# Output sums, row statistics and late norms moved between engines, scratch in PSUM, and another instruction order in a hybrid attention block

## Chip, cores and metric

The kernel runs on one core of a Trainium2 chip. The metric is the device time of one execution in microseconds (us); lower is better. A core has five engines that run their own instruction queues in order and wait for each other by semaphores: TensorE (PE; its weight loads are shown as PEld), VectorE (DVE), ScalarE (ACT), GpSimd (POOL) and SyncE (SP), which issues nearly all transfers here.

## What is computed

The reference applies four layers to `x` of shape 8 x 512 x 128, each added to its input after a layer norm over the 128 features. All is float32.

```python
x = x + attn_a(layernorm(x))   # delta rule, 16 heads of 8
x = x + ffn(layernorm(x))      # 8 experts, best 2 per token
x = x + attn_b(layernorm(x))   # linear attention, elu + 1, 16 heads of 8
x = x + ffn(layernorm(x))      # the same weights again

# attn_a: q, k, v = silu(short_conv(x @ W.T)), 4 taps; beta = sigmoid(x @ Wb.T)
# q, k divided by their norms over the 8 features of a head; then, token by token,
v_new = (v_t - k_t @ S) * b_t
S = S + outer(k_t, v_new)
o_t = q_t @ S
# o * rsqrt(mean(o * o) + eps) * o_norm_w, then @ Wo.T

# ffn: probs = softmax(x @ Wg); two largest, divided by their sum, as weights
h = relu(einsum('nd,edf->enf', xt, W1))    # 128 -> 256
y = einsum('enf,efd->end', h, W2)          # 256 -> 128
out = einsum('ne,end->nd', combine, y)

# attn_b: q, k = elu(x @ W.T) + 1; causal, with running sums S and z
out = (A @ v + q @ S) / (A.sum(-1) + q @ z + eps)   # A = tril(q @ k.T)
```

## The kernel before

**Tiling.** The 512 tokens of the eight sequences are cut into eight chunks `c` of 64 tokens. A chunk holds 64 tokens of all 8 sequences: 512 rows, kept as a tile of 128 partitions x 4 x 128 features. Chunk 7 goes through the later layers as two halves (`HALVED`).

**Stages of a chunk.** `prepare` (from L815) loads and normalizes the chunk, transposes it, projects it to q, k, v and beta, takes the short convolution (chunks 0 to 3 as four accumulated matmuls, later ones as three VectorE instructions for each of q, k, v, `s_pp_a<-cv_a`), and regroups the result to one sequence and head per partition through scratch in DRAM (`scr`, `qk`, `vv`). Norms of q and k come from `norms_of` (L877): squares on ScalarE, sums over a head by `over_heads` (four strip matmuls `s_pn_a`, a copy, a store `scn` and a load `nrm`), a clamp on GpSimd. `back` (L1020) and `substituted` (L1080) solve the delta rule within four steps, with a scratch tile `spare` and the result `W`.

`recurring` (L1176) is the sequential part: 16 steps per chunk, each of four VectorE instructions (`pj`, `factors`, `terms`, `st`). After every four steps `outputs` (L1235) multiplies the kept states by the queries on GpSimd (`po`, four instructions of 256 elements) and sums over the 8 features on VectorE (`o<-po`, 1024 to 128 elements); `SUMS_ON_PE`, empty here, names the chunks that would use TensorE instead. `ending` (L1296) corrects and normalizes the outputs (`on`) and sends them through DRAM (`sco`, `oT`) to be projected (`s_po_a`) and added to `x`.

`moe` (L1446) is a feed-forward layer, `f` the first and `g` the second. It transposes the rows, computes the routing logits (`narrow`, L778: four strip matmuls, one for each 128 tokens, then a copy and one transpose back), and then the routing on VectorE up to the weights `cb`. `relative` (L1518) turns the difference of the two largest logits into two weights with Exp. `all_experts` (L1354) sends `cb` to DRAM (`s_pw`, `cT`, `scw`), loads a row of it to all partitions for each expert (`wt_xsT<-scw`, 256 KB), multiplies by the transposed rows on GpSimd, and runs 16 matmuls `s_ph` with Relu on ScalarE (`hT`) and 16 accumulating matmuls `y_py`, all 512 wide. Expert 0 of chunks 0 and 7 is scaled before the transpose instead (`TURNED_IN`) and needs no load.

`linear_attention` (L1791) and `attend` (L1573) are attn_b. The row means come from strip matmuls (`s_pm_b`), a copy and a transpose, the variances from ScalarE squares (`inverse_deviation`, L760).

**Order.** Each engine's order is fixed when the program is built. A planner (`Weaver`, L153 on) runs all stages as streams against a table of durations (`duration`, L444) and at each step takes the stream whose remaining chain, plus a constant of its own from `FAVOURED` and `OFFSETS`, is longest. `PASSES` says how often the chains are computed anew. The first-come slots of `Slots` (L335) hand out tiles: five general PSUM banks (`banks`, L617), two for the feed-forward's sums and logits (`long_banks`), one for the recurrence. `keep_busy` (L1874) places filler matmuls (`busy`, L1885) of a matrix of ones in free banks where the planner sees TensorE idle for 0.6 us or more.

Every instruction issued through the planner has the line of its helper, L430, in the profile, so that the tiles' names are the way to read it. The expert weights 5 to 7 are loaded to `resident` only after chunk 3's projections, as their tiles hold the convolution's weights until then.

Of the kernel before, what the change touches and what calls it, by code (L numbers as in the profile page):

```python
# [42 lines left out]
SUMS_ON_PE = ()  # L43
# [3 lines left out]
ADDED_ON_DVE = (4,5,6,7)  # L47
KEPT_ON_DVE = (4,5,6)
# [14 lines left out]
PASSES = ((1, 0.0, {}), (17, 0.1, {}))  # L63

FAVOURED = {
    ("b", 0.0): 847, ("b", 1.0): -301, ("b", 2.0): 48, ("b", 3.0): -4, ("b", 4.0): -976, ("b", 5.0): -1159,
    ("b", 6.0): 509, ("b", 7.0): -2460, ("b", 7.5): 186, ("beside",): -125, ("ending",): 1282, ("f", 0):
    164, ("f", 1): -235, ("f", 2): -208, ("f", 3): 29, ("f", 4): 931, ("f", 5): -141, ("f", 6): -314, ("f",
    7): 1886, ("f", 7.5): -1425, ("g", 0.0): -218, ("g", 1.0): 61, ("g", 2.0): -140, ("g", 3.0): 611, ("g",
    4.0): 1326, ("g", 5.0): 199, ("g", 6.0): -1053, ("g", 7.0): -2296, ("g", 7.5): 1775, ("outputs",): -478,  # L70
    ("prepare", 0): -2816, ("prepare", 1): 490, ("prepare", 2): -322, ("prepare", 3): -911, ("prepare", 4):
    77, ("prepare", 5): -24, ("prepare", 6): 83, ("prepare", 7): -370, ("recur", 0): 2489, ("recur", 1):
    -593, ("recur", 2): 572, ("recur", 3): -1791, ("recur", 4): -302, ("recur", 5): -833, ("recur", 6):
    -3302, ("recur", 7): -653, ("values",): -814, None: -170,
# [4 lines left out]
    -94, -63, 10, -192, -39, 12, -114, -698, -137, 154, 81, -154, 130, -7, 6, -2, -25, -22, -2, 171, -146,  # L79
    -7, -70, 86, -128, -1, 17, -350, 642, -227, 85, -53, -408, -72, 354, -37, 34, -6, 645, -20, -144, 59,  # L80
    149, 52, 49, 18, 421, -76, -46, -60, 563, -491, 107, 160, -7, 102, -88, 28, 57, 480, -125, -15, -198,
    -41, -6, 81, 85, 0, 8, 24, -159, -105, 12, 78, -58, -26, -244, 80, -179, -12, 37, -10, 146, 131, 114,
    61, -165, 199, 28, 153, 232, 126, 187, 3, -64, -4, -68, -5, 154, -129, 405, 149, -77, -184, -114, 6,
    140, 71, 0, -30, 398, -30, 199, 51, 201, -31, -7, 93, 86, 98, 175, 3, 134, -160, 32, -8, 65, 39, 184,
    172, 22, -195, 62, -6, -117, -193, -21, 224, -2, 11, 349, 84, 127, 214, 76, -14, 19, -519, 30, 4, -176,
    -6, -26, -64, -20, 294, -16, -87, -219, 1, -473, -50, 39, -21, -282, -34, -184, 97, 149, -21, -158,
    -104, 106, 72, 0, 119, 19, 141, 62, 112, -108, 0, -120, -72, -44, 5, -107, -26, 0, -99, 88, 131, 88, 51,
    102, -9, -406, -123, 20, -48, -420, 9, 139, 52, -694, 192, 164, 383, 181, 63, 80, -29, 128, 63, 1, 144,
    196, 1, -34, 91, -132, -127, -70, 192, -19, -32, 65, 136, 236, 52, -67, -1, 15, -90, -28, 0, 2, 22, -94,
    -96, -15, 0, -15, -22, 99, 3, -43, -150, 46, 133, -168, 9, 53, 3, -72, 8, -173, 449, 96, 28, 122, -136,  # L90
    422, -272, 7, 434, 221, 71, -7, 29, -29, 153, 229, 84, -129, 5, 23, 279, 24, -90, -194, -16, -56, 427,
    89, -3, 1, -11, -603, -381, 204, 67, -10, -5, 0, -2, 45, -263, -472, -138, 30, 30, 82, 194, -1, -59,
    -23, -58, 0, 108, 62, -9, 5, -88, -5, -7, 18, -109, -19, 111, -199, -12, -202, 0, 89, 481, 420, -6,
    -211, 70, 51, -263, -17, 39, 141, 71, 4, -55, -254, 179, -98, 103, 36, -265, 132, -34, -36, -47, 41, 94,
    0, 12, -1, 146, 300, -7, 142, -45, 316, 3, -167, 2, -187, -134, -82, -567, 4, 37, 118, -22, 201, 80, 39,
    67, 63, -32, 260, -167, -29, -70, -55, -469, -372, -49, -2, 236, 0, 295, 102, 7, -41, 74, 9, -134, 43,
    -34, 188, -24, 140, -5, 429, 11, -94, 28, -42, 5, -15, -118, 87, -61, 20, 0, 475, 5, 16, -69, -126, 319,
    4, -99, 69, -4, 70, -87, 176, -124, -24, 435, 195, -54, 82, -79, 4, 720, -20, 54, 32, -167, 634, 242,
    -96, -30, -407, -108, -261, 56, -137, -130, 0, -300, 368, 33, 288, -490, 1, 22, -94, 42, 243, -58, 151,
    -49, 22, -272, 31, 845, 96, 0, 187, 208, -186, 12, 81, 23, -3, -487, -1188, 112, 246, 12, -243, -20,  # L100
    -207, 131, 0, 9, 1, 92, -154, -51, 0, -12, 174, 34, -129, 4, 60, 110, 27, 22, 67, -71, -22, -42, 59,
    210, 19, -55, 55, -152, 9, -15, -11, -151, 5, 0, -27, -47, 90, 461, 19, -340, -125, -548, -9, -32, -230,
    -61, -263, -69, 106, 281, 208, 173, 130, 24, -453, -25, -527, -530, 71, 63, 3, -54, 215, -207, 22, -48,
    -658, 219, 71, -172, -353, 11, -68, 60, -249, 0, 50, -22, 150, 6, -350, -52, 76, 30, -35, 557, 232,
    -368, -37, 275, -101, 150, 23, 282, 0, -780, 68, -85, 129, -425, 631, 106, 15, -121, 71, 30, 13, 0,
    -328, -24, 9, -98, -460, -5, -51, -90, 2, 20, 20, -105, -38, 87, 1, 0, -199, 99, 32, 89, 41, -98, 1,
    -272, -19, 2, -52, 181, 141, 243, 28, -31, -49, -72, 7, -71, -40, -24, 87, 8, -8, -51, -124, -5, 90,
    -63, -99, 264, 34, -87, 1, 92, 68, 55, -26, 299, -407, -12, 25, -346, 18, -21, -6, 44, 257, 0, 260,
    -223, -60, -27, 184, 47, 635, 14, -534, 0, 140, -70, -304, 223, 34, -48, 62, -166, -8, -102, -78, -30,
    103, -30, -960, -162, -66, -29, 50, -158, 711, 29, 291, 43, 14, 7, 92, -303, 27, 45, -809, 107, -64,  # L110
    138, 122, 0, -66, -98, -85, -58, 16, -414, -177, 106, -114, 45, 57, 51, 411, -98, -32, 16, 73, 321,
    -511, -85, 0, 397, 113, 54, 411, -4, 1, -51, 47, 414, 2, 166, 15, 92, 69, 58, -247, 30, 262, -1, 52,
    -212, -4, 18, -74, 98, 9, 30, -177, -203, -9, 10, 157, 31, 18, 29, -52, -10, -148, -8, 94, 228, 279, 77,
    2, 378, 636, -57, 159, 585, -108, -19, 247, 111, 562, 391, -2, 225, 13, -402, 143, -89, -146, -22, -185,
    -20, 132, -42, -70, 158, 1, 50, 37, -28, -167, -90, -210, 121, -233, -10, -66, 169, 191, 46, 36, -32,
    164, 68, 148, 540, -107, -33, -181, -38, -203, -36, 0, -147, 24, -545, -18, 89, -120, -91, -112, 569,
    -397, 90, -431, 640, -64, 17, -78, 12, -574, 0, 63, 16, -348, 271, 0, -12, -338, -270, -117, 29, -320,
    -188, -665, -232, 187, 43, -42, 130, -48, 66, -174, 22, 45, 51, 89, 11, 282, -21, 205, 433, -88, 263,
    -183, -149, 23, 0, -165, 22, -19, 116, 253, -89, -42, 80, 25, 8, -96, -35, -48, 22, 77, -33, 140, -44,
    0, -9, 65, -18, 87, 134, 104, 110, -25, 201, 0, 489, -110, 111, 35, 132, 96, 21, 26, 27, -33, -16, 10,  # L120
    20, -47, 28, 31, -10, -346, -6, 31, 72, -31, -124, 209, -70, 57, -329, -2, 164, 72, 25, 111, -22, -8,
    105, 297, 3, -394, 4, -68, 112, 104, 271, -203, 0, 2, 222, 24, 3, -55, -276, 94, -36, -222, -39, -139,
    41, 5, 126, -154, 82, 59, 40, 219, -79, 31, 117, 101, -104, -163, 0, -21, 140, 75, 13, 14, 27, 122, 63,
    201, -21, 0, 0, -86, -38, 79, -230, 330, 101, -77, 169, -15, -63, -74, 205, 6, -5, 11, 52, -8, -66, -5,
# [8 lines left out]
TABLES = ("exp", "silu", "sqrt")  # L133
TABLE_OF = {AF.Exp: "exp", AF.Tanh: "exp", AF.Silu: "silu", AF.Sqrt: "sqrt"}
# [24 lines left out]
class Weaver:  # L159
# [24 lines left out]
    def took(self, engine, us, lag=0.1, table=None, lands=0.0):  # L184
        free = self.clock.get(engine, 0.0)
        if engine == "PE":
            if table != self.mode:
                self.mode = table
                free += MODE
        elif table and table != self.table:  # L190
            self.table = table
            free += 1.3
# [68 lines left out]
    def run(self):  # L261
# [3 lines left out]
        def start(s):  # L265
            at, was_on, lag = s.state[:3]
            if isinstance(s.on, Event):
                return max(at + lag, s.on.at)
            engine = "ACT" if s.on in TABLES else s.on
            free = self.clock.get(engine, 0.0)  # L270
            switch = SWITCH if s.on in TABLES and s.on != self.table else 0.0
            at += lag if was_on != engine else after(engine)
            return max(at + switch, free + switch) if PENALTY else max(at, free + switch)
# [170 lines left out]
def duration(key, op, args, kw):  # L444
    if op == "dma_start":
        return key, 0.4, 0.0, None, LANDS
    if key == "PE":
        mode = args[0].shape[0], args[2 if op == "matmul" else 1].shape[0]
        mode = None if mode == (P, P) else mode
        if op == "transpose":  # L450
            return key, 0.115, 0.2, mode
# [42 lines left out]
def merged(  # L494
# [106 lines left out]
    nc.gpsimd.memset(mhalf, -0.5)  # L601

# [32 lines left out]
    hTs = held_in(3, [P, HB * P], "hT")  # L635
# [142 lines left out]
    def narrow(out, w, src, n):  # L778

        for g in range(n):  # L780
# [3 lines left out]
            if g:  # L784
                weaver.overlaps(0.15)

    def halves(out, w, src):

        for g in range(4):
# [3 lines left out]
            if g:  # L793
                weaver.overlaps(0.15)
# [1149 lines left out]
```

## Time and profile before

| what | value |
|---|---|
| median of three runs | 811.18 us (807.44, 811.18, 811.40) |
| the profiled execution, its time | 810.49 us |
| the profiled execution, first to last instruction (span) | 808.8 us |
| TensorE clock granted, mean | 0.973 |
| filler matmuls among TensorE's 757.4 us | 61.7 us, 227 matmuls |
| 512-wide expert matmuls, back to back | 0.86 us each |
| activation table loads | 30, 1283 ns each |

The page cuts the span in 40 slices of 20.2 us. In its second part each digit is the busy share of an engine in tenths, and PEclk is the clock that TensorE was granted:

```profile
DVE  1689997897999999889878897997625625442410
ACT  5665758767765667686857766766455555555443
POOL 1243545468658666774674668376805644446241
PEclk9998997799999999999999999999999999999999
```

VectorE is nearly full from the third slice to the fifteenth, and falls off after the recurrence of the last chunk, at some 560 us. In the groups of the profile, a line gives engine, operation, out and in tiles, shapes, the number of instructions, then total busy time, the mean of one, and the idle time of the engine ahead of them with what ended it.

### The profile page before, as it was taken

What the parts mean: (1) busy time and instruction counts of PE and PEld (TensorE: products, weight loads), DVE (VectorE), ACT (ScalarE), POOL (GpSimd) and SP (SyncE); (2) the same over time, 40 slices, a digit from 0 to 9 for tenths busy, and PEclk for the clock granted to TensorE, in tenths of its full rate; (3) what the DMA queues carried; (4) which work ended last, traced back from release to release, by engine and by line L of the source; (5) the groups of instructions that cost most, each with busy time, mean ns of one, the idle gap of its engine ahead of it and who ended that gap; (6) DMA issues with size and microseconds to landing.
All of it is one profiled execution on the core that took longest, in us unless ns stands there. A gap on an engine that the chain in (4) does not pass through costs nothing.

```text
span 808.8 us, 11447 instructions
## 1 busy us (share of the span) xinstructions
PE 757.4 (94%) x3321; PEld 371.3 (46%) x3321; DVE 575.2 (71%) x1425; ACT 512.3 (63%) x1434; POOL 446.0 (55%) x595
## 2 busy tenths in 40 slices
PE   8897895799888999999989999999999999999997
PEld 4343342343333444444534444444456545644476
DVE  1689997897999999889878897997625625442410
ACT  5665758767765667686857766766455555555443
POOL 1243545468658666774674668376805644446241
PEclk9998997799999999999999999999999999999999
DMA  2442442415521030222423224231401301303120
GB/s 45 118 124 52 125 106 59 125 40 132 133 65 55 1 94 25 80 79 80 118 72 91 93 45 141 70 106 37 108 1 47 106 21 39 106 1 99 40 76 23
DMA packets 84839, 60.24 MB, mean 74 GB/s; under 512 B 50600, under 2 KB 66600, under 8 KB 84776
## 3 DMA queue, kind: packets, MB, share of 16 engines
q1 hardware_dynamic: 84056, 59.23, 26.5%
q8 instruction: 26, 0.43, 0.2%
q10 hardware_dynamic: 720, 0.28, 0.2%
q14 instruction: 37, 0.30, 0.1%
HBM read 46.71 MB, written 12.78 MB: 74 GB/s over the span
## 4 chain that ended last, share of the span: by engine, by line
PE 71%; DVE 18%; ACT 3%; POOL 3%; issue 3%; DMA 2%; SPq 0%; DVEq 0%; ACTq 0%; POOLq 0%
PE s_ph_g L430 13%; PE y_py_g L430 13%; PE s_ph_f L430 11%; PE y_py_f L430 10%; PE s_pc_b L430 4%; PE s_pp_a L430 3%; PE busy L1885 3%; DVE spare L430 2%; DVE st L430 2%; DVE factors L430 2%; DVE W L430 2%; PE s_pu_b L430 2%; PE s_pp_b L430 2%; DVE pj L430 2%; DVE terms L430 2%
## 5 line engine op out<-in xcount | busy, mean ns | idle before, releaser
L430 PE MATMUL s_ph_f<-wt_xsT_f,resident 128*128 128x512 f32 (+1 forms) x288 | 135.9, 570 | 11.9 <-DVE on L430 4.5
L430 PE MATMUL y_py_f<-hT_f,resident 128*128 128x512 f32 (+1 forms) x288 | 137.3, 563 | 0.0
L430 PE MATMUL y_py_g<-hT_g,resident 128*128 128x512 f32 (+1 forms) x288 | 133.7, 552 | 0.1
L430 PE MATMUL s_ph_g<-wt_xsT_g,resident 128*128 128x512 f32 (+1 forms) x288 | 131.1, 553 | 0.6 <-POOL wt_xsT_g L430 0.4
L430 ACT ACTIVATE hT_g<-s_ph_g 128x512 f32<-128x512 f32 (+1 forms) x144 | 78.8, 548 | 82.7 <-PE s_ph_g L430 81.9
L430 ACT ACTIVATE hT_f<-s_ph_f 128x512 f32<-128x512 f32 (+1 forms) x144 | 78.2, 548 | 64.9 <-PE s_ph_f L430 64.1
L430 POOL TENSOR_TENSOR kv_b<-ph_b,v 128x1152 f32<-128x1152 f32 x32 | 69.8, 2194 | 55.5 <-ACT v L430 26.8
L430 POOL TENSOR_TENSOR wt_xsT_g<-wt_xsT_g,xn_xnT_g 128x512 f32<-128x512 f32 (+1 forms) x69 | 78.8, 1163 | 34.7 <-DMA wt_xsT_g<-scw_g 28.0
L430 POOL TENSOR_TENSOR po<-st,kq 128x256 f32<-128x256 f32 x128 | 91.5, 743 | 3.4 <-DVE y_pl_f L430 1.3
L430 POOL TENSOR_TENSOR wt_xsT_f<-wt_xsT_f,xn_xnT_f 128x512 f32<-128x512 f32 (+1 forms) x69 | 81.3, 1195 | 18.4 <-DMA wt_xsT_f<-scw_f 13.7
L430 PEld LDWEIGHTS s_ph_f<-wt_xsT_f,resident 128*128 128x128 f32 x288 | 52.1, 194 | 63.1 <-issue 35.6
L430 PEld LDWEIGHTS y_py_g<-hT_g,resident 128*128 128x128 f32 x288 | 51.1, 190 | 44.7 <-issue 33.7
L430 PEld LDWEIGHTS s_ph_g<-wt_xsT_g,resident 128*128 128x128 f32 x288 | 51.2, 190 | 43.9 <-issue 34.9
L430 PEld LDWEIGHTS y_py_f<-hT_f,resident 128*128 128x128 f32 x288 | 50.5, 193 | 44.3 <-issue 32.0
L1885 PE MATMUL busy<-ones 128*128 128x512 bf16 x227 | 61.7, 418 | 9.4 <-ACT narrow_bt_a L430 3.2
L430 DVE TENSOR_TENSOR qs_b<-s_pc_b,ph_b 128x360 f32<-128x360 f32 (+1 forms) x96 | 49.7, 552 | 26.9 <-PE s_pc_b L430 25.2
L430 DVE TENSOR_REDUCE st<-terms 128x64 f32<-128x320 f32 x128 | 61.7, 482 | 7.8 <-ACT terms L430 2.6
L430 DVE TENSOR_REDUCE factors<-pj 128x32 f32<-128x288 f32 x128 | 58.6, 458 | 4.0 <-ACT vn L430 1.2
L430 DVE TENSOR_TENSOR pj<-st,factors 128x256 f32<-128x256 f32 x128 | 53.6, 419 | 8.8 <-ACT factors L430 5.4
L430 ACT COPY terms<-st 128x64 f32<-128x64 f32 x128 | 39.4, 308 | 27.3 <-DVE st L430 26.8
L430 DVE TENSOR_TENSOR terms<-factors,kt 128x256 f32<-128x256 f32 x128 | 53.9, 421 | 3.8 <-ACT factors L430 1.3
L430 DVE TENSOR_REDUCE nd_b<-qs_b 128x90 f32<-128x720 f32 (+1 forms) x48 | 45.6, 950 | 0.7
(261 smaller groups left out, 1296.1 us busy)
## 6 DMA issues: line engine op xcount, KB each, us to landing
wt_xsT_f<-scw_f SPq DMA_DIRECT2D x55, 256.0 KB
wt_xsT_g<-scw_g SPq DMA_DIRECT2D x55, 256.0 KB
scr<-y_a SPq DMA_DIRECT2D x24, 256.0 KB
qk<-scr SPq DMA_DIRECT2D x16, 256.0 KB
x_a<-in_x_dram SPq DMA_DIRECT2D x16, 128.0 KB
vv<-scr SPq DMA_DIRECT2D x8, 256.0 KB
sco<-on SPq DMA_DIRECT2D x8, 256.0 KB
oT<-sco SPq DMA_DIRECT2D x8, 256.0 KB
```

Source lines behind the costliest of these rows:

```text
L430: r = call(*args, **kw)
L1885: nc.tensor.matmul(pt, ones, ones.unsqueeze(1).to_broadcast([P, 4, P]), start=True, stop=True)
```

## The change

Seven edits of the computation's placement come with a new set of planner constants:

- Chunks 0, 1 and 2 sum their outputs on TensorE: for each group of four steps, eight accumulating matmuls of an identity with every eighth element of `po`, and a copy by ScalarE, in place of one VectorE reduction.
- The substitution's scratch `spare` is one of the five general PSUM banks and no longer a tile in SBUF.
- Routing takes tanh of half the difference. The two weights are then one VectorE instruction each, with a factor `by` that GpSimd makes from the inverse deviation.
- Chunks 3 to 7 take the row statistics of attn_b from VectorE's `bn_stats` and `bn_aggr`, in place of strip matmuls, a transpose, copies and ScalarE squares.
- Chunks 5, 6 and 7 take both norms from the regrouped q and k: squares on ScalarE, a VectorE reduction and clamp, with no strip matmul and no transfer. Before, only the keys of chunk 0 did.
- Both feed-forwards of chunks 0 and 1 compute logits directly: four matmuls with the rows as weights and 32 columns moving, with no copy and transpose.
- `FAVOURED`, `OFFSETS` and `PASSES` are others, the planner's table knows that tanh is in two table sets, transposes no longer count as a mode of TensorE, and strip matmuls overlap by 0.185 in place of 0.15. So the order differs on every engine, and the number of fillers is 190 in place of 227.

```diff
-SUMS_ON_PE = ()
+SUMS_ON_PE = (0,1,2)
+NEAR_NORMS = (5,6,7)
+DIRECT = (0,1)
+STATS_ON_DVE = (3,4,5,6,7)
+PREPARED_ON_POOL = ()
+HIDDEN = 3
-PASSES = ((1, 0.0, {}), (17, 0.1, {}))
+PASSES = ((1, 0.0, {}), (3, 0.1, {}))
...
-TABLE_OF = {AF.Exp: "exp", AF.Tanh: "exp", AF.Silu: "silu", AF.Sqrt: "sqrt"}
+TABLE_OF = {AF.Exp: "exp", AF.Tanh: "tanh", AF.Silu: "silu", AF.Sqrt: "sqrt"}
+def served(table, by):
+    if table == "tanh":
+        return by if by in ("exp", "silu") else "exp"
+    return table
...
         if op == "transpose":
-            return key, 0.115, 0.2, mode
+            return key, 0.115, 0.2
...
-                weaver.overlaps(0.15)
+                weaver.overlaps(0.185)
...
-        def first_norms(k):
+        def near_norms(s, k):
...
             act.activation(flat, k.rearrange("p d t -> p (d t)"), AF.Square)
             yield "DVE"
+            dve.tensor_reduce(nrm[:, s], flat.rearrange("p (d t) -> p t d", d=HD), AX.X, ALU.add)
...
-                if c or s == 0:
+                if (c or s == 0) and c not in NEAR_NORMS:
                     spawn(norms_of(s, y))
...
-            if s == 1 and c == 0:
-                spawn(first_norms(qk[:, s]))
+            if s < 2 and (c in NEAR_NORMS or s == 1 and c == 0):
+                spawn(near_norms(s, qk[:, s]))
...
-            spare = pair.tile([P, CH, HD], F32, tag="spare", name=f"spare_{c}", bufs=1)
+            spares = yield from banks.take(f"spare_{n}")
+            spare = spares.rearrange("p (t d) -> p t d", d=HD)
...
+        if int(name[1]) in DIRECT:
+            for j in range(nb):
+                pe.matmul(
+                    pl[:, P + 32 * j : P + 32 * (j + 1)], xnT[:, j * P : (j + 1) * P], wg, start=True, stop=True
+                )
+        else:
...
+            scales["by"] = by = small.tile([P, 2, HB], F32, tag="by" + tag, name=f"by_{name}")[:, :, 0:nb]
+            pool.tensor_tensor(by, rs.unsqueeze(1).to_broadcast([P, 2, nb]), signs[:, :, 0:nb], ALU.mult)
...
-            act.activation(p2, apart, AF.Exp)
-            yield "DVE"
-            dve.tensor_scalar(wk[:, 0], p2, 1.0, None, ALU.add)
-            yield "DVE"
-            dve.reciprocal(wk[:, 0], wk[:, 0])
-            yield "DVE"
-            dve.tensor_tensor(wk[:, 1], p2, wk[:, 0], ALU.mult)
-            yield "DVE"
-            dve.tensor_tensor(wk, wk, rs.unsqueeze(1).to_broadcast([P, 2, nb]), ALU.mult)
+            yield "tanh"
+            act.activation(p2, apart, AF.Tanh, scale=0.5)
+            for k in range(2):
+                yield "DVE"
+                dve.scalar_tensor_tensor(wk[:, k], p2, 2.0 * k - 1.0, by[:, k], ALU.add, ALU.mult)
...
+        if on_dve:
+            seen = small.tile([P, HB, 6], F32, tag="seen" + tag, name=f"seen_{n}")
+            mv = small.tile([P, HB, 2], F32, tag="mv" + tag, name=f"mv_{n}")
+            for k in range(nb):
+                yield "DVE"
+                dve.bn_stats(seen[:, k], xt[:, k])
+            for k in range(nb):
+                yield "DVE"
+                dve.bn_aggr(mv[:, k], seen[:, k])
+            yield "POOL"
+            pool.tensor_scalar(rk[:, 0], mv[:, 0:nb, 1], LN_EPS, None, ALU.add)
+            pool.tensor_tensor(rk[:, 0], rk[:, 0], mhalf[:, 0:nb], ALU.pow)
```

The code that sums on TensorE was there before, unused:

```python
if c in SUMS_ON_PE:
    ps_o = yield from banks.take(f"po_{c}_{g}")
    sums = ps_o[:, 0 : SUB * TK * HD]
    terms_of = po.rearrange("p j s m d -> p (j s m) d")
    for d in range(HD):
        pe.matmul(sums, ident, terms_of[:, :, d], start=(d == 0), stop=(d == HD - 1))
    act.copy(to, sums.rearrange("p (j s m) -> p j s m", j=TK, s=SUB))
```

## The prediction

> **What bounds the kernel now.** I read the busy table of the page first, then the busy time in three stretches, the same for the filler matmuls alone, then the groups by shape and the waits of TensorE.
>
> ```profile
> PE 757.4 (94%) x3321; PEld 371.3 (46%) x3321; DVE 575.2 (71%) x1425; ACT 512.3 (63%) x1434; POOL 446.0 (55%) x595
> ```
>
> TensorE looks full over the whole span, but part of that is filler (`busy`, L1885), matmuls of ones that compute nothing. The cuts below are at the first expert matmul of chunk 0 (`s_ph_f`, 151.5 us) and at the first use of the second feed-forward's routing weights (`s_pw_g`, 291.5 us). The first answer is all work (us, PE, PEld, DVE, ACT, POOL busy, clock, DMA, GB/s), the second the fillers alone.
>
> ```profile
> 0.00:151.50 151.50, 124.51 (x535) 56.67 (x535) 115.58 (x293) 100.16 (x305) 60.69 (x126) 0.91 0.35 88
> 151.50:291.50 140.00, 123.37 (x522) 54.77 (x523) 127.74 (x291) 97.83 (x261) 92.05 (x115) 0.96 0.28 76
> 291.50:808.80 517.30, 509.52 (x2267) 259.84 (x2265) 331.88 (x843) 314.26 (x869) 293.23 (x356) 0.99 0.24 70
> ```
>
> ```profile
> 0.00:151.50 151.50, 58.86 (x217) 0.91 0.35 88
> 151.50:291.50 140.00, 2.23 (x8) 0.96 0.28 76
> 291.50:808.80 517.30, 0.59 (x2) 0.99 0.24 70
> ```
>
> So TensorE has in stage one 65.7 us of real work, 58.9 of filler and 27.0 idle; in stage two 121.1, 2.2 and 16.6; in stage three 508.9, 0.6 and 7.8. Stage three is bound by TensorE. Stages one and two are fed by VectorE: 91% busy in stage two, and in stage one 115.6 us busy although it has little to do in the first 25 us. The span is real work (695.7) + filler (61.7) + idle (51.4): time is won by real work that goes away in stage three, or by expert work that arrives sooner.
>
> ```profile
> L430 DVE TENSOR_REDUCE o<-po 128x128 f32<-128x1024 f32 x32 | 38.7, 1209 | 5.3 <-POOL po L430 5.3
> L430 DVE TENSOR_TENSOR W<-W,spare 128x512 f32<-128x512 f32 x21 | 18.7, 891 | 0.1
> L430 DVE TENSOR_TENSOR spare<-W,s_near_a 128x512 f32<-128x512 f32 x21 | 14.3, 682 | 0.1
> L430 DVE TENSOR_REDUCE nrm<-sq 128x64 f32<-128x512 f32 x1 | 1.1, 1082 | 14.6 <-ACT sq L430 14.6
> L430 DVE BATCH_NORM_STATS2 seen<-x_a 128x6 f32<-128x128 f32 x4 | 1.0, 284 | 4.0 <-DMA x_a<-in_x_dram 4.0
> ```
>
> ```profile
> L430 PE MATMUL s_po_a<-woa,oT 128*128 128x128 f32 x64 | 8.8, 278 | 0.4 <-DMA oT<-sco 0.4
> L430 PE MATMUL s_pn_a<-sq,heads 128*32 128x128 f32 x120 | 6.6, 294 | 5.4 <-ACT sq L430 5.2
> L430 PE MATMUL s_pm_b<-xn_xnT_b,wg 128*32 128x128 f32 x64 | 4.0, 283 | 0.0
> ```
>
> ```profile
> PE s_pn_a L430 <- ACT sq L430: 5.2, 2, 4.1
> PE s_ph_f L430 <- DVE on L430: 4.5, 1, 4.5
> ```
>
> In these rows a float32 matmul leaves two records, so `s_po_a` is 32 matmuls in 8.8 us, 0.275 each, and back to back 0.22 to 0.26 (four in 1.05). The 512-wide expert matmuls run at 0.86 (the chain of waits has 1.72 for two). `s_pn_a`, in four column strips, is 0.11 each, `s_pm_b` 0.125. The waits show single handoffs of 4 to 5 us at which TensorE had run dry.
>
> **Part by part, stage one.** By instruction order, the changed program puts before its first expert matmul 64 of the new sums (chunks 0, 1) and 53 fewer fillers, and moves behind it three 512-wide projections of chunk 4, two 256-wide weight matmuls, four transposes and twelve strip matmuls. Sums: 64 x 0.24 = +15.4. Moved: 3 x 0.86 + 2 x 0.43 + 4 x 0.23 + 12 x 0.11 + small ones 0.9 = -6.6. Real work 65.7 + 15.4 - 6.6 = 74.5; fillers 164 x 0.271 = 44.5 (0.271 = 58.86/217). Together 119.0, before any idle.
>
> VectorE: ahead of the first `cb_f` (146.9 us, 111.9 us busy until then) its queue loses eight `o<-po` reductions (8 x 1.21 = 9.7), eight steps of chunk 2's recurrence (four instructions of 0.48, 0.46, 0.42, 0.42, one of them once less: 13.9), eight convolution taps of chunk 4 (8 x 0.75 = 6.0) and 4.9 of chunk 1's end and scratch: 34.5 by mean durations. The whole list adds to 130 by means where the trace has 111.9 busy, as neighbours overlap, so 34.5 x 0.86 = 30 us; `cb_f` could be ready at 117. Between `s_pw_f` and the first expert matmul stand now 11 us of TensorE work (four projections 3.4, 16 sums 3.8, transposes, strips, a weight matmul and four fillers 3.4); in the timeline of before it took 4.3. So the first expert matmul comes at about 130: 119.0 + 11 idle instead of 27. Of VectorE's 34.5 the sums are 9.7; the rest is order. What moves forward with routing 0: its four `scw` stores and seven broadcast loads on SP, among `resident` loads and chunk 3's scratch, and one `m_xs_f` product on POOL among chunk 1's `po`. In the timeline of before the first load was issued 7.2 us after `s_pw_f`, and its matmul came 15.6 us after it. The 11 us and the four matmuls of expert 0, which needs no load, cover this chain: cost 0, up to 4.5 (the longest single wait above) if they don't.
>
> The sums add a wait: VectorE waited for `po` four times, 5.3 us, and now TensorE does, with the next projections or experts behind it, which VectorE's scratch and ScalarE's Relus wait for. Twelve groups at 1.3 would be 16; 18 us of idle are left in stages one and two for it, so I add nothing.
>
> **Stage two.** TensorE: 32 sums, 7.7; three projections of chunk 4 +2.6, weight matmuls, transposes and strips +2.7, three expert matmuls -2.6, eight `s_pc_b` -1.6, four transposes and routing -1.5: 121.1 + 7.3 = 128.4; fillers 14 x 0.28 = 3.9. VectorE between `cb_f` and `cb_g`: four `o` reductions fewer (-4.8) and 5.9 of scratch and attention less, but seven recurrence steps (+13.0), eight taps (+6.0) and 3.9 of norms and small ones more: +12.2 by means, +10.5 busy. From 117: 131.4 + 10.5 + 8 to 13 idle (13.2 before) = 267 to 272; TensorE from 130: 132.3 gives 262 plus idle. I take 269 for `s_pw_g`, 22.5 sooner than 291.5, with 7 us idle in this stage.
>
> **Stage three.** Row statistics on VectorE for chunks 3 to 7 take 20 strip matmuls and six transposes of `s_pm_b` away (-3.9), late norms 16 strip matmuls (-1.8), direct logits 1.0; three expert matmuls, eight `s_pc_b` and four transposes come in from before the cut (+5.1): -1.6. Ten more fillers +2.7; eight of them and a gap of about 1.3 stand in front of the last half chunk's experts, whose routing now has 5.6 us of other matmuls to hide behind. VectorE gains 20 `seen` x 0.284 + 20 `mv` x 0.154 + 4 norms x 0.7 to 1.1 less the routing's two instructions per feed-forward: +11.9 by means, +10 busy in 517 where it has 185 idle: price 0 if the idle takes it, 10 if it all falls on the last chunks' recurrence. That cover is thin up to chunk 7's end (234.6 busy of 278.5 between 291.5 and 570), so I take 3. 517.3 - 1.6 + 2.7 + 1.3 + 3 = 522.7.
>
> **The other edits.** Scratch in PSUM: `W<-W,spare` with both inputs in SBUF takes 891 ns, `spare<-W,s_near_a` with one in PSUM 682; 21 x 0.21 = 4.4 less, counted above. But `spare` holds one of five general banks while a chunk is substituted; price 0 to 12 us (a bank wait of 0.5 at each of 24 expert matmuls that run beside two substitutions), taken 0, since each matmul's bank is emptied by one 0.6 us Relu. Twelve copies of sums on ScalarE at 0.28 = 3.4, hidden in 296 us of idle; routing by tanh drops a reciprocal and two products and adds one small POOL product (0.2); twelve fewer DMAs on SP. The new order has 33 table loads where there were 30: 3 x 1.28 = 3.9 on ScalarE, hidden. [...]
>
> **The price of a sum.** Its moving operand steps 32 bytes; no row of before has such a step. Bounds: 0.11 (a strip matmul) and 0.86 (a 512-wide one); I take 0.24 as it is nearest in shape to `s_po_a`. [...]
>
> **Sum.** 269 + 522.7 = 792, against the profiled span of 808.8. That execution took 810.5; the median of the runs is 811.18, 2.4 over the span. 792 + 2 = 794.
>
> **Rivals.** *Strided sums are dear* (slower): 96 x (p - 0.24), less some 18 us of idle and slack in the first two stages. At 0.86: 59.5 - 18 = +41, 835. It decides from p = 0.6, where 34.6 - 18 eats the gain. Against it: TensorE takes 0.86 for 512 float32 columns, 1.7 ns for each, slow enough to leave a read some room. Chance 0.06. *The order doesn't do what it says*: TensorE's idle stays at 51.4 because it is paid at handoffs, as in the waits above; then real work 15.4 - 6.6 + 7.3 - 1.6 = +14.5 and fillers -37 x 0.27 = -10 make 813, run time 816. For it: most of the idle that I remove is not tied to one wait. Against it: the fillers fall by 37 and the routing of chunk 0 is queued eight recurrence steps sooner. Chance 0.07. *Given back late*: the statistics and norms fall on the path to chunk 7 with all their 10 (7 more than taken) and the scratch's bank costs half of its 12: 792 + 13 = 805, run 807. For it: VectorE's 84% up to 570; against it: TensorE there has the experts of two or three chunks in hand. Chance 0.12. *Front at full gain*: TensorE's idle in stages one and two falls to 6, as VectorE's list allows: 792 - 12 = 780, run 782. Chance 0.17.
>
> **Numbers.** Forecast 794, 0.58, its own range 785 to 803. The range 779 to 809 takes in the full front gain and the late loss, and leaves out the dear sums and the unchanged idle. About 0.5% (4 us) is what a measurement can tell from no change: faster than 807: 0.58 + 0.17 + half of the late loss = 0.81; within, its other half and a little of the unchanged idle: 0.08; slower: 0.11.
>
> **What would show it.** First `s_ph_f` near 130 and first `s_pw_g` near 269; fillers about 45 us before the first; `s_po<-po` at 0.22 to 0.28; `W<-W,s_spare_a` near 690; TensorE idle after 269 under 15 us. Wrong if `s_ph_f` starts after 142, if a sum is over 0.5, or if TensorE waits often for `x_a` or `on` in stage three.

## The result and the profile after

The changed kernel takes 813.77 us (median of 11 runs, 812.68 to 814.76), the kernel before in the same comparison 809.11 (11 runs). The ratio is 1.0053, with a 95% interval of 1.0040 to 1.0066: a loss of 3 to 5 us, where a gain to 794 had been forecast. The profiled execution's span is 813.1 us.

The busy table comes first, then the busy time in three stretches, cut where the prediction cut the kernel before: at the first expert matmul `s_ph_f` (now 136.2 us) and at the first use of the second routing weights `s_pw_g` (289.9). The columns are PE, PEld, DVE, ACT and POOL busy with their instructions, granted clock, DMA share and GB/s. The third fence has the fillers alone.

```profile
PE 780.3 (96%) x3378; PEld 402.9 (50%) x3378; DVE 573.5 (71%) x1429; ACT 503.6 (62%) x1387; POOL 442.9 (54%) x609
```

```profile
0.00:136.20 136.20, 126.66 (x564) 71.37 (x565) 96.38 (x253) 81.76 (x242) 51.39 (x106) 1.00 0.35 92
136.20:289.90 153.70, 140.46 (x593) 71.19 (x591) 130.69 (x296) 114.52 (x326) 95.29 (x138) 0.97 0.28 73
289.90:813.10 523.20, 513.17 (x2223) 260.29 (x2223) 346.44 (x881) 307.31 (x819) 296.26 (x367) 1.00 0.23 69
```

```profile
0.00:136.20 136.20, 40.64 (x164) 1.00 0.35 92
136.20:289.90 153.70, 4.00 (x14) 0.97 0.28 73
289.90:813.10 523.20, 3.08 (x12) 1.00 0.23 69
```

TensorE's busy time less the fillers gives its real work, and the stretch less the busy time its idle time:

| stretch | length, forecast | length, measured | real work, forecast and measured | filler | idle, forecast and measured |
|---|---|---|---|---|---|
| to the first expert | 130 | 136.2 | 74.5, 86.0 | 44.5, 40.6 | 11, 9.5 |
| to `s_pw_g` | 139 | 153.7 | 128.4, 136.5 | 3.9, 4.0 | 7, 13.2 |
| to the end | 522.7 | 523.2 | 510.6 with the fillers, 513.2 | | 12, 10.0 |

The length of the last stretch came out as forecast, though with 2.6 us more work and 2 us less idle time than forecast. What is missing stands in the first two stretches, and most of it is real work of TensorE. The groups of the page name it:

```profile
L453 PE MATMUL s_po<-po,ident 128*128 128x128 f32 x192 | 47.2, 414 | 1.4 <-POOL po L453 1.4
L453 DVE TENSOR_REDUCE o<-po 128x128 f32<-128x1024 f32 x20 | 24.2, 1210 | 1.9 <-POOL po L453 1.9
L453 DVE TENSOR_TENSOR W<-W,s_spare_a 128x512 f32<-128x512 f32 x21 | 14.3, 683 | 0.4
L453 ACT COPY o<-s_po 128x128 f32<-128x128 f32 x12 | 3.2, 265 | 21.8 <-PE s_po L453 21.8
```

The 96 sums are 192 records and take 47.2 us, 0.49 each (0.24 had been taken). ScalarE's twelve copies of the sums stood 21.8 us in front of them: TensorE, not VectorE, was now late. The scratch in PSUM did what was forecast (683 ns where 891 had been). The timeline just before the first expert matmul (start, length, engine, group) shows the size beside its neighbours:

```profile
122.09 3.60 PE L453 MATMUL s_pp_a<-xnT_a,resident 128*128 128x512 f32 x8
125.53 3.89 PE L453 MATMUL s_po<-po,ident 128*128 128x128 f32 x16
...
132.42 3.98 PE L453 MATMUL s_po<-po,ident 128*128 128x128 f32 x16 [0.58 <-POOL po L453]
136.22 1.90 PE L453 MATMUL s_ph_f<-wt_xsT_f,resident 128*128 128x512 f32 x4
```

Eight sums of 128 columns take 3.9 us back to back, more than four projections of 512 columns. Two groups stand between `s_pw_f` at 122.0 and the first expert, where the forecast had 3.8 us for both.

### The profile page after: what moved, and what is told of

It is laid out like the page before. It is cut to its first block, busy times and chain, and to the rows that moved or that the text cites. A ratio compares the mean times of both kernels' runs of the same rounds, so it can differ in the third digit from the quotient of the medians.

```text
span 813.1 us, 11588 instructions
## 1 busy us (share of the span) xinstructions
PE 780.3 (96%) x3378; PEld 402.9 (50%) x3378; DVE 573.5 (71%) x1429; ACT 503.6 (62%) x1387; POOL 442.9 (54%) x609
## 4 chain that ended last, share of the span: by engine, by line
PE 70%; DVE 13%; ACT 5%; issue 4%; POOL 4%; DMA 2%; DVEq 0%; SPq 0%; POOLq 0%; ACTq 0%
PE y_py_g L453 12%; PE s_ph_g L453 12%; PE s_ph_f L453 11%; PE y_py_f L453 10%; PE s_po L453 5%; PE s_pc_b L453 4%; PE s_pp_a L453 3%; POOL po L453 2%; DVE st L453 2%; PE s_pp_b L453 2%; PE s_pu_b L453 2%; DVE factors L453 2%; DVE terms L453 2%; PE busy L1937 1%; PE s_pS_b L453 1%
## 5 line engine op out<-in xcount | busy, mean ns | idle before, releaser
L453 PE MATMUL y_py_f<-hT_f,resident 128*128 128x512 f32 (+1 forms) x288 | 134.8, 557 | 1.2 <-ACT hT_f L453 1.2
L453 POOL TENSOR_TENSOR po<-st,kq 128x256 f32<-128x256 f32 x128 | 90.1, 732 | 16.1 <-PE s_po L453 10.3
L453 PEld LDWEIGHTS y_py_f<-hT_f,resident 128*128 128x128 f32 x288 | 51.7, 191 | 50.5 <-issue 39.7
L453 PEld LDWEIGHTS s_ph_f<-wt_xsT_f,resident 128*128 128x128 f32 x288 | 50.4, 192 | 48.4 <-issue 31.2
L453 DVE TENSOR_REDUCE st<-terms 128x64 f32<-128x320 f32 x128 | 61.5, 481 | 14.5 <-ACT terms L453 7.6
L453 PEld LDWEIGHTS y_py_g<-hT_g,resident 128*128 128x128 f32 x288 | 50.5, 190 | 39.2 <-issue 31.9
L1937 PE MATMUL busy<-ones 128*128 128x512 bf16 x190 | 47.7, 386 | 3.5 <-DVE qs_b L453 1.8
L453 PE MATMUL s_po<-po,ident 128*128 128x128 f32 x192 | 47.2, 414 | 1.4 <-POOL po L453 1.4
```

What stands on the lines that cost most here:

```text
L453: r = call(*args, **kw)
L1937: nc.tensor.matmul(pt, ones, ones.unsqueeze(1).to_broadcast([P, 4, P]), start=True, stop=True)
```

## The experiments

In every variant of the changed kernel the instructions on all five engines stand in the same order as in the changed kernel, except where an edit says otherwise; the same holds for the variants of the kernel before. So a difference is the edit's and not a new plan's.

**The step of a sum's operand.** In `dense` GpSimd writes its products so that the eight terms lie in eight blocks, and each sum reads 128 elements in a row; in `steps` (a single execution) they lie 8 bytes apart in chunk 0, 16 in chunk 1 and 32 in chunk 2, and GpSimd writes the first two chunks in smaller instructions.

```diff
+ laid = flat.rearrange("p (d j s m) -> p j s m d", j=TK, s=SUB, m=HD)
- pool.tensor_tensor(po[:, 2 * i + j], st[:, i : i + SUB], queries, ALU.mult)
+ pool.tensor_tensor(laid[:, 2 * i + j], st[:, i : i + SUB], queries, ALU.mult)
- pe.matmul(sums, ident, terms_of[:, :, d], ...)
+ pe.matmul(sums, ident, flat[:, d * 128 : (d + 1) * 128], ...)
```

> GpSimd writes po of chunks 0 to 2 with the summed index outermost, so that each sum's matmul reads 128 elements side by side and no longer one in eight (32 bytes apart). Same instructions, same order. Theory 1 (the step makes a sum dear, and TensorE is the bound from 40 us on): s_po falls from 0.47 to 0.22-0.25 us a matmul, 47 to some 22-24 us in all, and the span by nearly as much, from 813 to 789-795. Rival 2 (the front is set by VectorE and by handoffs): the sums get cheap, TensorE idles instead, span 805-813. Rival 3 (the price is that of accumulating eight matmuls, not of the step): s_po stays at 0.47, span 813. If GpSimd's strided writes cost much more than 0.73 us each, up to 48 x that is added in front of the sums.

> A measurement only: the sums of chunk 0 read elements 8 bytes apart, those of chunk 1 16 bytes apart, those of chunk 2 32 bytes apart as in the changed kernel (GpSimd writes the first two in more and smaller instructions, which is slower). [...] Rival 3: 0.47 at all three.

`dense` takes 799.84 us (799.3 to 801.76), a ratio of 0.9882 to the kernel before (0.9861 to 0.9903), and beats both kernels. The price fell nearly as far as the first theory expected (0.26 where it had 0.22 to 0.25); the span, 797.6, lies between the ranges of the first two theories, and the third theory, on accumulation, is out. Its groups and stretches:

```profile
L454 PE MATMUL s_po<-po,ident 128*128 128x128 f32 x192 | 25.3, 288 | 4.1 <-POOL po L454 4.1
L454 ACT COPY o<-s_po 128x128 f32<-128x128 f32 x12 | 3.2, 266 | 4.8 <-PE s_po L454 4.7
```

```profile
0.00:127.90 127.90, 111.78 (x564) 59.46 (x565) 95.84 (x252) 81.42 (x242) 49.46 (x104) 1.00 0.37 93
127.90:274.50 146.60, 134.02 (x594) 65.82 (x592) 132.02 (x298) 114.54 (x326) 97.31 (x140) 0.97 0.30 80
274.50:797.60 523.10, 513.16 (x2223) 260.56 (x2223) 346.44 (x881) 307.04 (x819) 296.27 (x367) 1.00 0.23 69
```

The same 96 matmuls take 25.3 us, 0.26 each, in place of 47.2, and ScalarE waits 4.7 us for them in place of 21.8. Of the 21.9 us saved 15.5 show in the span; most of the rest is TensorE's idle time, which grows by 5.8 (38.6 against 32.8): slack that the dear sums had used. In the timeline of `steps` a group of eight sums is one line; the four are two of chunk 0, one of chunk 1 and one of chunk 2:

```profile
50.55 1.98 PE L454 MATMUL s_po<-po,ident 128*128 128x128 f32 x16
...
81.09 1.98 PE L454 MATMUL s_po<-po,ident 128*128 128x128 f32 x16
...
102.89 3.79 PE L454 MATMUL s_po<-po,ident 128*128 128x128 f32 x16
...
145.99 3.89 PE L454 MATMUL s_po<-po,ident 128*128 128x128 f32 x16
```

At 8 bytes a sum costs 0.25 us, at 16 bytes 0.47, at 32 bytes 0.49, all at a granted clock of 1.00. So the price is that of the operand's step, and it nearly doubles between 8 and 16 bytes. What in the chip makes it so, no run shows.

**The fillers.** In `fewfill` (the changed kernel) and `dense_fewfill` the fillers that the planner puts after 30 us aren't issued: 46 of 190 stay. In `dense_late` only the 26 behind the first expert matmul fall away.

```diff
+ if at < 30.0:        # 150.0 in dense_late
      pt = ps.tile([P, 4, P], F32, tag=f"s{i}", name="busy")
      for _ in range(n):
          nc.tensor.matmul(pt, ones, ...)
```

> The fillers planned after 30 us are not issued, all else and the whole order stay. Theory 1: TensorE is full in the front, so fillers that lie in no gap push the sums and projections; some 30 us of them go, first expert matmul from 136 to 118-128, span 795-805. Rival 2 (the front is fed by VectorE): first expert matmul at 130-136, span 809-813. Rival 4 (the clock falls when TensorE goes idle): granted clock under 0.95 before 160 us, projections and sums longer, span 813-830.

> Both edits together. Theory 1 alone with TensorE still the bound: 770-785. If VectorE becomes the bound once TensorE has room: no faster than the better of the two, 787-795. Rival 4: slower than the contiguous sums alone by the lower clock.

> Densely laid sums (799.8), and the 26 fillers after the first expert matmul left out (14 between it and the second routing weights, 12 in front of the last experts); the 164 fillers before it stay. Theory 'fillers pay only where TensorE has little work': the first stage keeps its clock of 1.00, the last stage loses the 2 us by which it was shorter in both runs without fillers, 796 to 799. Rival 'every filler holds the clock for what follows it': 800 to 803.

`fewfill` takes 818.49 us (ratio 1.0101, 1.0085 to 1.0118), `dense_fewfill` 804.91 (0.9937, 0.9916 to 0.9957): each about 5 us slower than with its fillers, though 35 us of filler work are gone. That is what the rival on the clock expected of `fewfill`; the first theory, a gain, is out for both. Two slices of 40 us of the changed kernel, then of `fewfill`, with the clock as the third figure from the end:

```profile
40.00:80.00 40.00, 39.15 (x176) 22.01 (x175) 33.98 (x76) 24.23 (x74) 18.44 (x33) 1.00 0.29 76
80.00:120.00 40.00, 38.58 (x176) 23.09 (x175) 34.88 (x90) 24.82 (x81) 14.10 (x26) 1.00 0.31 80
```

```profile
40.00:80.00 40.00, 31.25 (x116) 18.83 (x115) 30.71 (x71) 23.01 (x72) 17.77 (x32) 0.71 0.30 76
80.00:120.00 40.00, 30.69 (x133) 20.26 (x131) 33.59 (x79) 23.31 (x80) 14.20 (x26) 0.80 0.30 76
```

Without fillers the granted clock falls to 0.71 and 0.80, TensorE's real work grows from 732.6 us to 748.8 (761.3 - 12.5), and VectorE has less done in the same time (30.7 us of work against 34.0). `dense_late` takes 798.21 us (797.45 to 799.5; ratio 0.9858, 0.9842 to 0.9875), inside what its theory expected, but its interval overlaps that of `dense`: that the late fillers cost 1 to 2 us isn't settled. As leaving out the late ones loses nothing, the fillers that earn their place are those of the first stage.

**The sums back on VectorE.** In `sums_dve` the planner still counts the sums, but each group is one VectorE reduction at that place.

```diff
- for d in range(HD):
-     pe.matmul(sums, ident, terms_of[:, :, d], ...)
+ nc.vector.tensor_reduce(to, po, AX.X, ALU.add)
- act.copy(to, sums...)
```

> The changed program with only its 96 sums taken back: the twelve groups are added by twelve VectorE reductions again, issued at the place of the sums; every other instruction and its place is as in the changed kernel. TensorE loses 47.2 us of work, VectorE gains 12 x 1.21 = 14.5 ahead of the first use of the second routing weights. Theory 'VectorE feeds the first two stages': what VectorE gains shows, 10 to 14 us over the 799.8 of the densely laid sums: 810 to 814, the same as the changed kernel, so that strided sums gave back all that taking them off VectorE had won. Rival 'TensorE sets the first two stages in this order': time falls with TensorE's work, 785 to 797.

It takes 814.78 us (814.52 to 815.18; ratio 1.0060, 1.0045 to 1.0075), just above what the first theory expected: 47 us less on TensorE and 14.5 more on VectorE leave the time where it was. Its first two stretches:

```profile
0.00:136.20 136.20, 106.64 (x436) 48.95 (x436) 101.26 (x254) 80.43 (x235) 48.15 (x102) 0.91 0.33 85
136.20:290.90 154.70, 133.13 (x527) 59.47 (x527) 138.26 (x308) 112.98 (x321) 98.55 (x143) 0.91 0.29 78
```

VectorE carries 12.4 us more than in the changed kernel up to that point (239.5 against 227.1), TensorE is idle for 51 us, and the stretches end at the same times, 136.2 and 290.9. So beside this kernel strided sums win nothing, and dense ones win 15 us. That all of it is VectorE's relief is not shown, for a second thing changes with it: with more idle time TensorE's granted clock is 0.91 in both stretches (1.00 and 0.97 in the changed kernel), and its work other than fillers and sums takes 696.4 us (752.6 - 56.2) in place of 685.4 (780.3 - 47.7 - 47.2). A run that takes the sums off TensorE and holds its clock wasn't made.

**The scratch back in SBUF.** `dense_sbuf` is `dense` with `spare` as an SBUF tile again; its bank stays set aside, and the statistics' scratch `seen` is one tile in place of six to make room.

```diff
  spares = yield from banks.take(f"spare_{n}")
- spare = spares.rearrange("p (t d) -> p t d", d=HD)
+ spare = pair.tile([P, CH, HD], F32, tag="spare", ..., bufs=1)
- seen = small.tile([P, HB, 6], F32, tag="seen" + tag, ...)
+ seen = small.tile([P, HB, 6], F32, tag="seen", ...)
```

> Densely laid sums, and the substitution's scratch back in SBUF (the general bank is still set aside, so the order stays; the statistics' scratch is one tile in place of six to make room). VectorE's product of two SBUF inputs 891 ns in place of 683 and the product into the scratch back near its old price: 4 to 5 us of VectorE work more, of which 3 to 4 stand ahead of the second routing weights. Theory 'VectorE feeds the first two stages': 801 to 805. Rival 'VectorE's work is hidden behind TensorE': 799 to 800.5, as with the scratch in PSUM.

It takes 804.55 us (803.4 to 806.24; ratio 0.9935, 0.9915 to 0.9956), 4.7 more than `dense`. Of `dense_sbuf` and then of `dense`:

```profile
L454 DVE TENSOR_TENSOR W<-W,spare 128x512 f32<-128x512 f32 x21 | 18.7, 890 | 0.4
L454 DVE TENSOR_TENSOR spare<-kq,W 128x256 f32<-128x256 f32 x14 | 12.6, 917 | 0.1
```

```profile
L454 DVE TENSOR_TENSOR W<-W,s_spare_a 128x512 f32<-128x512 f32 x21 | 14.3, 683 | 0.4
L454 DVE TENSOR_TENSOR s_spare_a<-kq,W 128x256 f32<-128x256 f32 x14 | 10.4, 740 | 0.2
```

VectorE's two products cost 6.6 us more (4.4 and 2.2), and 4.7 come out, inside what the first theory expected. `s_pw_g` is 2.4 us later (276.9 against 274.5) and the part after it 3.8 longer (526.9 against 523.1), so the scratch pays behind the second cut too, which the theory hadn't placed there. GpSimd is busy 5.6 us longer as well (448.6 against 443.0), so how the 4.7 divide between the two engines isn't shown. What the bank costs was not tried alone.

**The sums in the old order.** `before_sums` is the kernel before with 11 of the 12 groups summed on TensorE from dense products, at the place of the reduction (at the twelfth no bank is free); `before_strided` reads them at 32 bytes.

```diff
- dve.tensor_reduce(to, po, AX.X, ALU.add)
+ for d in range(HD):
+     nc.tensor.matmul(sums, ident, flat[:, d * 128 : (d + 1) * 128], ...)
+ nc.scalar.copy(to, sums...)
```

> The kernel before, in its own order, with 11 of the 12 groups of chunks 0 to 2 summed on TensorE from densely laid products; nothing else is changed. TensorE +11 x 1.95 = 21 us in stages with 27 and 17 us idle and 59 us of filler, VectorE -11 x 1.21 = -13.3, ScalarE +3. Theory 'VectorE feeds the first two stages': 797 to 803. Rival 'the new order makes the gain': 807 to 811, as the old order has nothing ready to fill the time that VectorE leaves.

> The same with the sums read at the step of 32 bytes, as the change has them: TensorE another 11 x 1.94 = 21 us. Theory 'a strided sum costs 0.47 to 0.49 us and VectorE feeds the first two stages': 8 to 15 us more than with dense products, 806 to 815. Rival 'the old order has idle time and fillers enough to hide the dear sums': within 3 us of the dense ones.

Both theories on `before_sums` missed: 830.71 us (829.8 to 831.56; ratio 1.0256, 1.0240 to 1.0272), 21 slower than before. `before_strided` takes 850.34 (848.15 to 850.69; 1.0500, 1.0483 to 1.0518), another 19.6, about the 18.8 us that its sums take more; that is above both of its expectations too. Of `before_sums` and then of `before_strided`:

```profile
L1298 PE MATMUL po<-po,ident 128*128 128x128 f32 x176 | 24.6, 299 | 9.6 <-POOL po L431 9.6
L1301 ACT COPY o<-po 128x128 f32<-128x128 f32 x11 | 2.9, 265 | 26.2 <-PE po L1298 26.2
```

```profile
L1293 PE MATMUL po<-po,ident 128*128 128x128 f32 x176 | 43.4, 415 | 9.5 <-POOL po L431 9.4
L1296 ACT COPY o<-po 128x128 f32<-128x128 f32 x11 | 2.9, 265 | 44.6 <-PE po L1293 44.6
```

TensorE is idle for 50.5 us (828.0 - 777.5), as in the kernel before (51.4): none of its idle time took the sums in. And ScalarE stands 26.2 and 44.6 us in front of their copies. Three more runs asked whether that wait or the fillers were the cause: in `before_swap` each group takes the next eight fillers away (74 in all), in `before_dvecopy` VectorE copies the sums, and `before_swap_dvecopy` has both.

```diff
+ OWED[0] += 8                          # before_swap, at each group
- for _ in range(n):                    # where fillers are placed
+ less = min(OWED[0], n)
+ OWED[0] -= less
+ for _ in range(n - less):
- nc.scalar.copy(to, sums...)           # before_dvecopy
+ nc.vector.tensor_copy(to, sums...)
```

> The kernel before in its own order with the 11 densely laid groups of sums on TensorE (830.7), and for each group the next eight fillers are left out: 74 of the 227 fall away, all after the first sum. Theory 'the old order has fillers where the sums would have to stand, and a filler that is issued is never skipped': TensorE loses 74 x 0.27 = 20 us, the time falls by 15 to 22, to 808 to 816, or to 800 where VectorE's saving of 13 shows as well. Rival 'the copies of the sums hold up ScalarE and by it the recurrence' (ScalarE stood 26 us before them): less than 6 us of it comes back, 824 to 831.

> The same 11 groups with all the old order's fillers, but the summed group is copied from PSUM by VectorE, at the place where the reduction stood, and not by ScalarE. Rival theory 'the copies hold up ScalarE': the 20 us come back for the most part, 805 to 815. Theory 'the fillers stand in the way': 824 to 834, as VectorE now waits for the same sums.

> Both at once: 74 fillers fewer and the copies on VectorE. If the two causes add, this is the lowest of the three, 798 to 808, and shows what the sums alone, densely laid, are worth in the old order; if the fillers are the whole cause it is as the first; if the copies are, as the second.

They take 824.22 us (ratio 1.0195, 1.0177 to 1.0212), 828.27 (1.0246, 1.0228 to 1.0265) and 823.04 (1.0179, 1.0155 to 1.0204), where 798 to 808 had been expected of the third if the causes add. Neither cause is the main one. Without 74 fillers 17.4 us of filler work go (59.1 to 41.7), but TensorE's idle time grows from 50.5 to 59.5, and its real work by 3.1 (718.4 to 721.5). The fillers are no clean test, as the clock falls with them: 0.91 and 0.93 in the first two stretches (cut at 157.9 and 307.0 us), where `before_sums` has 0.93 and 0.94 (cut at 162.7 and 311.8). And when VectorE copies, VectorE waits. Two lines of the waits of `before_dvecopy` (engine, what waited and for whom, us, times, longest):

```profile
PE po L1298 <- POOL po L431: 10.2, 6, 3.0
DVE o L1301 <- PE po L1298: 29.7, 11, 4.8
```

What is shown is that the sums don't pay when they are only put where the reduction stood: the chain GpSimd, TensorE, copy is one handoff longer, and whichever engine takes the copy waits 2.4 to 2.7 us for each group. The chain of work that ended last shows where it is lost: in `before_sums` all 11 groups stand in it, with 7.5% of its first 320 us, 24 of the 24.6 us that they take; in `dense` 7 of the 12 groups do, with 5.0% of its first 290 us, 14.5 of 25.3. So in the old order next to nothing of the sums is hidden, in the new one some 11 us. Why the old order hides none wasn't found.

## Why the prediction was wrong, step by step

- **The price of a sum: the step that failed.** The prediction had bounds of 0.11 and 0.86, took 0.24 "as it is nearest in shape", and wrote of the step that no row of before has one. Dense sums cost about that (0.26), strided ones 0.49, which is still under the 0.5 that it named as a sign of being wrong. The sum's term was 96 x 0.24 = 23; the measured one is 47.2, 24.2 more. With it TensorE's real work is 732.6 us, where the prediction's terms give 695.7 + 14.5 = 710.2; in `dense` it is 710.5. Span: 792 + 22.4 of real work - 4 of fillers + 3 of idle = 813.
- **The reason given for the low price** was that TensorE takes 1.7 ns for each float32 column of a wide matmul, "slow enough to leave a read some room". That was an estimate, and a column of the strided sums took more than twice as long: 3.7 ns at 16 bytes and 3.8 at 32 (0.47 and 0.49 us over 128).
- **The rival "Strided sums are dear"** named the right cause, the step, and put its turning point too high. It gave 18 us of idle time and slack to swallow the sums, so that it would decide only from 0.6. The comparison of `dense` with the changed kernel shows 6 of 22 us swallowed, so a price of 0.49 already lost.
- **The idle time of the second stretch** was taken as 7 us and is 13.2 after and 12.6 in `dense` (146.6 - 134.0). With the price of the sums put right it is most of what is left: `dense` has a span of 797.6 where 792 was forecast. The waits for `po`, counted as nothing, are 4.1 us on TensorE in `dense`, over both stretches.
- **The first stretch** is right in its sum once the sums are cheap, `s_ph_f` at 127.9 in `dense` for 130, but by parts that cancel: real work 71.2 for 74.5, fillers 40.6 for 44.5 and idle 16.1 for 11. The prediction had no term for the clock. It is 0.91 there before and 1.00 after, and a filler falls from 0.271 us to 0.248 (40.6/164), which over 164 fillers is the 3.9 that they came out lower; for the real work the same cause is likely, and not shown.
- **The third stretch** was right, 523.2 for 522.7, its two misses cancelling. TensorE's idle time, 32.8 where some 30 was forecast, is right by luck: the dear sums fill part of it, and at the price that the forecast took it is 38.6 (`dense`). The rival "The order doesn't do what it says" (816) came near the time for a wrong reason: it kept idle at 51.4.
- **"Of VectorE's 34.5 the sums are 9.7; the rest is order"**: in the new order moving the sums to TensorE, densely laid, is worth 15 us (`sums_dve` against `dense`, with what the clock does), in the old order it costs 21. So the two parts can't be added up separately; of these two orders the move pays only in the one planned for it.
- **Scratch in PSUM** at 4.4 us of VectorE work and a price of nothing for its bank: these products gain 6.6 and 4.7 us show; the price of the bank stays open. The other edits (row statistics, late norms, tanh, direct logits) were tried only together with the new order, so what each is worth isn't known.

## What to carry to other kernels

Before a reduction is given to TensorE as a sum over strided slices, look at the step in bytes and let the producer write the terms in blocks: here that cost GpSimd 10 ns in 730 and nearly halved the time of the sums (47.2 to 25.3 us). Where an unknown price has bounds a factor of eight apart, take the price at which the plan breaks as a case with real weight, and work that point out from measured slack. Plan the order for a moved operation: here it paid in the order made for it and lost when it was only put in the old place.

## What the runs showed of the hardware

- A float32 matmul of 128 columns took 0.24 to 0.26 us when its moving operand (`po`) stepped 4 bytes (`dense`: eight back to back in 1.95 us, a mean of 0.26) or 8 (`steps`, 0.25), 0.47 at 16 bytes (`steps`) and 0.49 at 32 (`steps` and the changed kernel). Between 16 and 32 bytes there is next to nothing.
- GpSimd's 256-element product took 730 ns (mean up to 160 us) when it wrote its results in a row, and 740 when neighbouring results went 512 bytes apart.
- With the fillers of ones the granted clock was 1.00 in 40 to 120 us; without them (`fewfill`) it was 0.71 in the first half of that and 0.80 in the second, and the kernel 5 us longer, with 35 us of filler work less.
